# A scheduled state-space kernel: the scan pass's bfloat16 splits get a cost of their own in the planner

## The chip, the cores and the metric

The kernel runs on one core of a Trainium2 chip. The metric is the device time of one execution in microseconds (us). The core has five engines that run side by side, each with its own queue of instructions in order: TensorE (PE, matrix products and transposes), VectorE (DVE), ScalarE (ACT), GpSimd (POOL) and SyncE (SP), which issues the DMA transfers here.

## What is computed

A state-space image layer, followed by an attention and a quantized feed-forward layer, on `x` of 8 x 64 x 64 x 96. The scan pass, which the change touches, computes a selective scan over 4096 tokens in four directions (K = 4), for 192 channels, each with 16 states. Cut to what matters:

```
x_dbl = einsum('bkdl,kcd->bkcl', xs, x_proj_weight)       # 6 + 16 + 16 rows
dts, Bs, Cs = x_dbl[:, :, :6], x_dbl[:, :, 6:22], x_dbl[:, :, 22:]
delta = softplus(einsum('bkrl,kdr->bkdl', dts, dt_projs_weight) + bias)
h = h * exp(delta_t * A) + (delta_t * u_t) * B_t           # for each t, 16 states
y_t = sum over the states of h * C_t
y = y + D * u
```

Everything is float32. The rows `dts` and `Bs` enter matrix products as sums of three bfloat16 parts[...]: the first part is the value rounded to bfloat16, the second the rounded rest, the third the rest of that.

## The kernel before

There are three passes. Pass 1 normalizes, projects, convolves and makes `x_dbl`, which it stores as `xd_d`. Pass 2, the scan pass, is most of the time. Pass 3 is the gate, the attention and the feed-forward layer.

The order of instructions is not the order of the source. Each unit of work is a Python generator that, before each of its steps, yields an engine, an estimated cost in us, and sometimes a delay until the result can be used and a buffer that it needs. The function `weave` (from L142) plays the units against these costs: at each turn it takes, of all open units, the step that can begin first (`key = (max(begin, free[engine]), rank)`, ties by a rank that is a due time), and only then are its instructions written out. The engines later execute these lists in order; what the costs were then no longer plays a part, but the order that they made does.

The scan pass has 192 pieces: 4 pairs of batches, 3 channel groups c (two of 128 channels of one batch, and c = 2, which holds the last 64 channels of both), 4 directions k, and 4 stretches of T = 1024 tokens. A piece has 16 states n, each with these steps:

- ScalarE makes the decay `da` (exp of delta times A), in one of 3 buffers.
- The input term `dbu` is made in a PSUM buffer `wide` (3 of them) in one of three ways: ScalarE scales `duT` into `x` and TensorE transposes it; or GpSimd scales it into `xg` and TensorE transposes that; or TensorE spreads B over the partitions and VectorE multiplies by `du`.
- VectorE scans, two states into one `h` buffer (3 of them).
- GpSimd multiplies a pair of states by `c`, the rows of C that a DMA has spread over the partitions (6 buffers of 1 MB).
- TensorE transposes and sums the products into `acc`.

Once a piece, `prepare` loads the bfloat16 parts (`xdt`, `xb`) and `u`, and makes `delta`, `du` (GpSimd) and `duT`.

The generator `split` (L234) makes the three parts of `dts` and `Bs`. One split loads a tile `bq` of 128 x 512 (or 96 x 512) float32 from `xd_d`; ScalarE casts it into part 0 of `bs`; GpSimd subtracts that from `bq`; ScalarE casts the rest into part 1; GpSimd writes the last rest as part 2; SyncE stores `bs` in two transfers, into `b_d` or `dt_d`. Each batch needs 2 x 3 = 6 splits. Those of batches 0 to 4 (`b < LATE`, with LATE = 5) belong to pass 1 (L523) and have two buffers for each tile. Those of batches 5 to 7, 18 of them, are `late_split` units of the scan pass (L624 to 627) with one buffer each, one split open at a time, and a due time of five pieces for each split: the rank is `5 * N * (i + 1)`. They are wanted by the pieces of pair 2, which begin with piece 96 (`yield "split", b` in `prepare`).

The lines that the change and the prediction touch: the two `yield "pool", 4.4` in `split` (L245, L249), its signature (L234), and its two calls (L523, L626). The costs of the other steps on GpSimd in the scan pass are 4.55 for `times_c`, 2.5 for `scaled_by_pool` and 2.37 for `du`.

Of the kernel before, what the change touches and what calls it, by code (L numbers as in the profile page):

```python
# [230 lines left out]
    return a_neg, dsum, dt_b, dt_w, sel, sel2  # L231


def split(engines, pool_of, src, row, rows, pieces, at, dst):  # L234

    act, pool, sp = engines
    wide, used = GRP, rows * pieces
    yield "sp", 0.7, 4.0
    bq = pool_of.tile([P, wide], F32, name="bq")
    src = src[row : row + rows].rearrange("r (s t) -> (r s) t", s=pieces)  # L240
    sp.dma_start(bq[0:used], src[:, at : at + wide])
    yield "act", 0.6
    bs = pool_of.tile([P, NS, wide], BF16, name="bs")
    act.copy(bs[0:used, 0, :], bq[0:used])
    yield "pool", 4.4  # L245
    pool.tensor_sub(bq[0:used], bq[0:used], bs[0:used, 0, :])
    yield "act", 0.6
    act.copy(bs[0:used, 1, :], bq[0:used])
    yield "pool", 4.4  # L249
    pool.tensor_sub(bs[0:used, 2, :], bq[0:used], bs[0:used, 1, :])  # L250
    yield "sp", 0.9
    half = used // 2
    for k2 in range(2):
        to = dst[k2].rearrange("e n (s t) -> (n s) e t", s=pieces)[:, :, at : at + wide]
        sp.dma_start(to, bs[half * k2 : half * (k2 + 1)])


def splits(b, o, b_d, dt_d):

    return [(0, 2 * N, 4, at, b_d[b][o]) for at in (0, GRP)] + [(DT0, 2 * R, 8, 0, dt_d[b][o])]  # L260
# [3 lines left out]
def pass1(ctx, tc, g, consts, ident, mhalf, engines, u_d, z_d, xd_d, b_d, dt_d):  # L264
    nc = tc.nc
    pe, dve, act, pool = engines
    sp = InOrder(tc, nc.sync)
# [3 lines left out]
    two = ctx.enter_context(tc.tile_pool(name="p1two", bufs=2))  # L271
# [24 lines left out]
    def later_loads():  # L296
        load_by_type(act, conv_w, g["conv_w"])
        load_by_type(act, conv_b, g["conv_b"])
        w0 = 0
        for rows in (slice(R, R + N), slice(R + N, NXD), slice(0, R)):  # L300
            wide = rows.stop - rows.start
            for k2 in range(2):
                src = slice(k2 * NXD + rows.start, k2 * NXD + rows.stop)
                act.dma_start(w_xp[:, 0, :, w0 : w0 + wide], g["x_projT"][0:P, :, src])
                for j in range(2):
                    act.dma_start(w_xp[64 * j : 64 * j + 64, 1 + j, :, w0 : w0 + wide], g["x_projT"][P:DI, :, src])
                w0 += wide
# [28 lines left out]
    def statistics(b, q):  # L336
        if b > 1:
            yield "proj", b - 2
        yield "sp", 0.6, 4.0
        x = transposed(three, "xs", b, q)  # L340
        next(x)
        yield "pe", 0.7, 0.3, pts
        pt, slot = next(x), pts.taken
        end = yield "dve", 0.7
        if b not in sts:
            sts[b] = two.tile([C, NG, 6], F32, name="st")
        dve.bn_stats(sts[b][:, q, :], pt[0:C, :])
        pts.release(slot, end)
        one_more(("st", b), NG, end)

    def group_norm(b):

        yield "st", b
        yield "dve", 0.2
        mv = two.tile([C, 2], F32, name="mv")
        dve.bn_aggr(mv, sts[b].rearrange("p a b -> p (a b)"))
        yield "pe", 0.3, 0.3, mms
        pm, slot = ps_mm.tile([P, GRP], F32, name="pm", tag="mm"), mms.taken
        pe.matmul(pm[0:C, 0:1], gmat, mv[:, 0:1], start=True, stop=True)
        end = yield "dve", 0.5  # L360
        mms.release(slot, end)
        gm = wp.tile([C, 2], F32, name=f"gm{b}")
        dve.tensor_copy(gm[:, 0:1], pm[0:C, 0:1])
        dq = two.tile([C, 1], F32, name="dq")
        dve.tensor_sub(dq, mv[:, 0:1], gm[:, 0:1])
        dve.scalar_tensor_tensor(dq, dq, dq, mv[:, 1:2], ALU.mult, ALU.add)
        yield "pe", 0.3, 0.3, mms
        pv, slot = ps_mm.tile([P, GRP], F32, name="pv", tag="mm"), mms.taken
        pe.matmul(pv[0:C, 0:1], gmat, dq, start=True, stop=True)
        end = yield "dve", 0.2  # L370
        mms.release(slot, end)
        dve.tensor_copy(gm[:, 1:2], pv[0:C, 0:1])
        yield "pool", 1.0
        pool.tensor_scalar(gm[:, 1:2], gm[:, 1:2], 1e-5, None, ALU.add)
        pool.tensor_tensor(gm[:, 1:2], gm[:, 1:2], mhalf[0:C, 0:1], ALU.pow)
        end = yield "dve", 0.2
        dve.scalar_tensor_tensor(gm[:, 0:1], gm[:, 0:1], -1.0, gm[:, 1:2], ALU.mult, ALU.mult)
        gms[b] = gm
        done["stats", b] = end
# [98 lines left out]
    def x_projection(b, o, q):  # L478
        pair, j = b // 2, b % 2
        yield "u", pair, j  # L480
        yield "u", pair, 2
        px = None
        for ty, u in ((0, us[pair, j]), (1 + j, us[pair, 2])):
            end = yield ("pe", 0.62, 0.4) if px else ("pe", 0.62, 0.4, pxs)
            if px is None:
                px, slot = ps_px.tile([P, GRP], F32, name="px", tag="px"), pxs.taken
            if o == 0:
                src = u[:, q * GRP : (q + 1) * GRP]
            else:

                src = u.rearrange("p (h w) -> p h w", w=WW)[:, :, q * RPG : (q + 1) * RPG]
            pe.matmul(px, w_xp[:, ty, o, :], src, start=ty == 0, stop=ty > 0)
        one_more(("xproj", b), 2 * NG, end)
        by_dve = b == NB - 1 and q % 2 == 1
        end = yield ("dve" if by_dve else "act"), 0.6 if o == 0 else 0.8
        xd = four.tile([2 * NXD, GRP], F32, name="xd")
        src, dst = px[0 : 2 * NXD, :], xd
        if o == 1:
            src, dst = src.rearrange("p (h w) -> p w h", w=RPG), xd.rearrange("p (w h) -> p w h", w=RPG)
        (dve.tensor_copy if by_dve else act.copy)(dst, src)  # L500
        pxs.release(slot, end)
        end = yield "sp", 0.9, 3.0
        sp.dma_start(xd_d[b][o][:, q * GRP : (q + 1) * GRP], xd)
        one_more(("xd", b, o), NG, end)

    def after(key, unit):
        yield key
        yield from unit

    units = []  # L510
    for pair in range(NB // 2):
        batches = (2 * pair, 2 * pair + 1)
        for b in batches:
            units += [("stats", statistics(b, q)) for q in range(NG)]
            units.append(("norm", group_norm(b)))
            units += [("proj", projection(b, q)) for q in range(NG)]
        for c in ORDER:
            units.append(("conv", convolution(pair, c)))
        for b in batches:
            for o in range(2):  # L520
                units += [("xproj", x_projection(b, o, q)) for q in range(NG)]
                if b < LATE:
                    units += [("split", after(("xd", b, o), split((act, pool, sp), two, xd_d[b][o], *w))) for w in splits(b, o, b_d, dt_d)]  # L523
    later_loads()
    room = {"proj": 4, "norm": 1, "stats": 3, "xproj": 4, "split": 2, "conv": 3}
    weave([(kind, (list(room).index(kind), i), unit) for i, (kind, unit) in enumerate(units)], room, done)
# [3 lines left out]
def pass2(ctx, tc, g, ident, engines, fixed, u_d, xd_d, b_d, dt_d, y_d):  # L530
# [3 lines left out]
    pe, dve, act, pool = engines  # L534
    sp = InOrder(tc, nc.sync)
    one = ctx.enter_context(tc.tile_pool(name="p2one", bufs=1))
    two = ctx.enter_context(tc.tile_pool(name="p2two", bufs=2))
# [6 lines left out]
    pieces = [  # L544
        (pair, c, k, NPC - 1 - i if k >= 2 else i) for pair in range(NB // 2) for c in range(3) for k in range(K) for i in range(NPC)
    ]
# [6 lines left out]
    def one_more(key, of, end):  # L553
        counts[key] = counts.get(key, 0) + 1
        if counts[key] == of:
            done[key] = end
# [66 lines left out]

    def late_split(b, o, which):  # L624

        yield from split((act, pool, sp), one, xd_d[b][o], *which)  # L626
        one_more(("split", b), 6, 0.0)

    def load_c(at, m):
# [187 lines left out]
    units = []  # L817
    for at, (pair, c, k, pc) in enumerate(pieces):
# [21 lines left out]
        add("acc", 0, take_acc(at), N)  # L840
    last = [(b, o, w) for b in range(LATE, NB) for o in range(2) for w in splits(b, o, b_d, dt_d)]
    units += [("split", 5 * N * (i + 1), late_split(*which)) for i, which in enumerate(last)]
    weave(units, {"prep": 1, "c": 1, "da": 2, "x": 1, "xg": 1, "dbu": 2, "scan": 2, "carry": 1, "term": 1, "sum": 1, "acc": 1, "split": 1}, done)

# [285 lines left out]
```

## Time and profile before

| | us |
|---|---|
| median of 3 runs | 10572.03 |
| lowest and highest | 10562.71, 10575.15 |
| the profiled execution | 10581.88 |
| its span, first to last instruction | 10580.1 |
| scan pass in it, first scan to end of last scan | 762.6 to 9673.4 |

The page gives one profiled execution. A group line reads: line of the source (here always that of a helper, L91), engine, operation, output <- inputs, shapes, count | busy time in us, mean of one in ns | idle time of the engine just before, and what ended most of it. The view of stretches gives, for each, the length, and then for PE, the PE weight loads, DVE, ACT and POOL the busy time and the count, then the granted TensorE clock as a share of full speed, the DMA share and GB/s. A wait line reads: who waited <- for what: us in total, times, longest.

### The profile page before, as it was taken

The numbers are of one execution on the slowest core, as the hardware profiler recorded it, in microseconds if no ns is written. First come the engines' busy times: TensorE is split into PE (matmuls) and PEld (weight loads), VectorE is DVE, ScalarE is ACT, GpSimd is POOL, SyncE is SP. The second block draws the span as 40 slices with busy tenths as digits, with TensorE's granted clock in tenths as the row PEclk, the third lists the DMA queues.
The fourth block names the chain that finished last, engine by engine and source line by source line (L and its number), as shares of the span: only waits on it lengthen the run. The fifth ranks groups of instructions, "written<-read, shape, count | busy, mean of one in ns | idle before, by whom it ended". The sixth has DMA issues, their size and how long they took to land.

```text
span 10580.1 us, 151226 instructions
## 1 busy us (share of the span) xinstructions
PE 7655.9 (72%) x51232; PEld 6290.1 (59%) x51232; DVE 9604.6 (91%) x6918; ACT 9346.2 (88%) x21427; POOL 9230.7 (87%) x3271
## 2 busy tenths in 40 slices
PE   6857777766777777777677777777777777766887
PEld 3326666665566666666566666665566666655775
DVE  6869999988999999999999999999999999997776
ACT  5759999989999999999999999999999999996665
POOL 1539999988999999999999999999999999997886
PEclk8879898988889899988999999988999999897776
DMA  5766676678886666698966666899766667887442
GB/s 150 237 188 209 201 221 209 213 197 190 200 213 208 211 217 210 214 205 195 212 216 206 219 213 214 206 200 204 216 210 210 219 208 217 198 197 181 127 125 64
DMA packets 928007, 2103.20 MB, mean 199 GB/s; under 512 B 274391, under 2 KB 422648, under 8 KB 925700
## 3 DMA queue, kind: packets, MB, share of 16 engines
q1 hardware_dynamic: 919812, 2092.79, 70.8%
q8 instruction: 410, 6.72, 0.3%
q14 instruction: 361, 2.96, 0.1%
q10 hardware_dynamic: 7424, 0.74, 0.1%
HBM read 1917.59 MB, written 175.66 MB: 198 GB/s over the span
## 4 chain that ended last, share of the span: by engine, by line
ACT 29%; DVE 22%; issue 17%; PE 16%; POOL 11%; DMA 4%; SPq 1%; DVEq 0%; ACTq 0%; POOLq 0%
DVE h L91 16%; ACT x L91 13%; ACT da L91 11%; POOL c L91 7%; PE acc L91 6%; PE wide L91 6%; DVE wide L91 4%; PE mm L91 2%; ACT L91 1%; DMA xd_d<-xd 1%; DVE u L91 1%; ACT delta L91 1%; POOL xg L91 1%; PE pa L91 1%; ACT duT L91 1%
## 5 line engine op out<-in xcount | busy, mean ns | idle before, releaser
L91 POOL TENSOR_TENSOR c<-c,h 128x2048 f32<-128x2048 f32 x1536 | 6970.4, 4551 | 449.2 <-DVE h L91 380.8
L91 DVE TENSOR_TENSOR_SCAN h<-da,carry,wide 128x1024 f32<-128x1024 f32 x2304 | 5259.4, 2332 | 272.6 <-PE wide L91 187.6
L91 ACT ACTIVATE x<-duT,bT 128x128 f32<-128x128 f32 (+1 forms) x14336 | 4162.8, 367 | 45.9 <-PE wide L91 40.4
L91 ACT ACTIVATE da<-delta,a_neg 128x1024 f32<-128x1024 f32 x3072 | 3508.5, 1145 | 398.1 <-DVE h L91 385.7
L91 PE MATMUL acc<-ident,c 128*128 128x128 f32 x24576 | 3509.4, 300 | 466.5 <-POOL c L91 435.3
L91 PEld LDWEIGHTS acc<-ident,c 128*128 128x128 f32 x24576 | 3185.5, 156 | 780.9 <-POOL c L91 609.2
L91 PE MATMUL wide<-ident,x 128*128 128x128 f32 x11264 | 1631.5, 293 | 852.4 <-DVE h L91 826.9
L91 PEld LDWEIGHTS wide<-ident,x 128*128 128x128 f32 x11264 | 1358.7, 150 | 1150.2 <-DVE h L91 503.1
L91 DVE TENSOR_TENSOR_SCAN h<-da,wide 128x1024 f32<-128x1024 f32 x768 | 1710.0, 2272 | 128.9 <-PE wide L91 79.1
L91 DVE TENSOR_TENSOR wide<-du,wide 128x1024 f32<-128x1024 f32 x1216 | 1461.9, 1212 | 117.8 <-PE wide L91 115.9
L91 PE MATMUL wide<-xb,sel 96*128 96x512 bf16 x2432 | 763.3, 399 | 574.6 <-DVE h L91 491.4
L91 POOL TENSOR_TENSOR xg<-duT,bT 128x512 f32<-128x512 f32 (+1 forms) x640 | 892.2, 1409 | 57.6 <-PE wide L91 42.6
L91 PE MATMUL wide<-ident,xg 128*128 128x128 f32 x3584 | 519.3, 292 | 282.8 <-DVE h L91 273.1
L91 PEld LDWEIGHTS <-sel 96*128 96x128 bf16 x2432 | 225.1, 101 | 749.3 <-issue 366.9
L91 PEld LDWEIGHTS wide<-ident,xg 128*128 128x128 f32 x3584 | 431.1, 151 | 357.1 <-issue 203.6
L91 POOL TENSOR_TENSOR du<-delta,u 128x1024 f32<-128x1024 f32 x192 | 454.9, 2369 | 187.4 <-ACT delta L91 179.8
L91 ACT ACT_TABLE_LOAD x385 | 494.0, 1283 | 6.8
L91 DVE SCALAR_TENSOR_TENSOR u<-xpad,conv_w,u 128x4096 f32<-128x4096 f32 x96 | 459.1, 4782 | 1.9
L91 PE MATMUL px<-u,w_xp 128*128 128x512 f32 x512 | 255.7, 642 | 75.6 <-ACT u L91 45.4
L91 PE MATMUL mm<-w_out,gt 128*128 128x96 f32 (+1 forms) x1024 | 261.0, 375 | 35.0 <-POOL gt L91 16.3
L91 PE MATMUL wide<-ident,du 128*128 128x128 f32 x1536 | 212.4, 284 | 76.3 <-DVE h L91 53.5
L91 PEld LDWEIGHTS mm<-w_out,gt 128*128 128x128 f32 (+1 forms) x1024 | 199.9, 241 | 98.0 <-issue 31.7
(132 smaller groups left out, 5874.5 us busy)
## 6 DMA issues: line engine op xcount, KB each, us to landing
c<-xd_d SPq DMA_DIRECT2D x1024, 1024.0 KB
c<-xd_d SPq DMA_DIRECT2D x1024, 512.0 KB
u<-u_d SPq DMA_DIRECT2D x128, 512.0 KB
xdt<-dt_d SPq DMA_DIRECT2D x1152, 36.0 KB
xb<-b_d SPq DMA_DIRECT2D x384, 96.0 KB
u<-u_d SPq DMA_DIRECT2D x128, 256.0 KB
y_d<-y SPq DMA_DIRECT2D x24, 1024.0 KB
y<-y_d SPq DMA_DIRECT2D x64, 384.0 KB
```

The costliest lines, as they stand in the source:

```text
L91: ins = getattr(self.engine, op)(*args, **kwargs).ins
```

## The change

`split` takes the cost of its two GpSimd steps as an argument. Pass 1 gives the 4.4 that stood there; the scan pass gives 1.25. The instructions that `split` issues are the same.

```
-def split(engines, pool_of, src, row, rows, pieces, at, dst):
+def split(engines, pool_of, cost, src, row, rows, pieces, at, dst):
...
-    yield "pool", 4.4
+    yield "pool", cost
     pool.tensor_sub(bq[0:used], bq[0:used], bs[0:used, 0, :])
...
-    yield "pool", 4.4
+    yield "pool", cost
     pool.tensor_sub(bs[0:used, 2, :], bq[0:used], bs[0:used, 1, :])
...
-                    units += [("split", after(("xd", b, o), split((act, pool, sp), two, xd_d[b][o], *w))) for w in splits(b, o, b_d, dt_d)]
+                    units += [("split", after(("xd", b, o), split((act, pool, sp), two, 4.4, xd_d[b][o], *w))) for w in splits(b, o, b_d, dt_d)]
...
-        yield from split((act, pool, sp), one, xd_d[b][o], *which)
+        yield from split((act, pool, sp), one, 1.25, xd_d[b][o], *which)
```

## The prediction

> **What bounds the kernel now.** I read the page first, then the busy times of each engine in stretches, then the waits of VectorE in two of those stretches, then the groups that touch the split's tiles. From the page:
>
> ```profile
> PE 7655.9 (72%) x51232; PEld 6290.1 (59%) x51232; DVE 9604.6 (91%) x6918; ACT 9346.2 (88%) x21427; POOL 9230.7 (87%) x3271
> ...
> DVE 6869999988999999999999999999999999997776
> ...
> L91 POOL TENSOR_TENSOR c<-c,h 128x2048 f32<-128x2048 f32 x1536 | 6970.4, 4551 | 449.2 <-DVE h L91 380.8
> L91 DVE TENSOR_TENSOR_SCAN h<-da,carry,wide 128x1024 f32<-128x1024 f32 x2304 | 5259.4, 2332 | 272.6 <-PE wide L91 187.6
> ```
>
> Three engines are near 90% over the span, and the scan pass (slices 3 to 37) is flatter still. VectorE leads. The scan pass is 192 pieces of 16 scans, twelve stretches of 16 pieces: four pairs of batches, each with channel groups c = 0, 1, 2. I cut the trace at the first scan of each stretch (762.5 us for the first). The view of stretches, with the columns PE, PE loads, DVE, ACT, POOL (busy us and count), granted PE clock, DMA share and GB/s:
>
> ```profile
> 762.50:1505.20 742.70, 536.17 (x3818) 465.94 (x3819) 695.10 (x358) 690.91 (x1499) 686.47 (x187) 0.89 0.65 204
> 1505.20:2249.30 744.10, 540.66 (x3845) 474.42 (x3844) 698.74 (x361) 685.89 (x1496) 688.25 (x188) 0.88 0.68 211
> 2249.30:3051.60 802.30, 554.15 (x3754) 474.77 (x3753) 718.04 (x377) 744.52 (x1982) 723.59 (x249) 0.86 0.88 197
> 3051.60:3785.60 734.00, 526.74 (x3835) 454.82 (x3833) 694.91 (x361) 679.92 (x1473) 683.31 (x183) 0.91 0.68 212
> 3785.60:4505.90 720.30, 526.28 (x3841) 444.63 (x3840) 692.42 (x361) 677.93 (x1481) 676.70 (x178) 0.93 0.67 214
> 4505.90:5267.90 762.00, 543.36 (x3758) 459.89 (x3756) 715.34 (x377) 738.66 (x1971) 713.29 (x240) 0.89 0.90 203
> 5267.90:5989.30 721.40, 523.25 (x3834) 442.14 (x3835) 692.62 (x361) 675.79 (x1466) 676.33 (x177) 0.94 0.67 214
> ```
>
> The reader is to see that stretches 5, 6 and 7 repeat themselves: 720 to 722 us for c = 0 and 1, 762 us for c = 2, and the later pairs do the same. The first four are longer: by 742.7-720.3 = 22.4, 744.1-721.5 = 22.6 (721.5 is stretch 8), 802.3-762.0 = 40.3 and 734.0-720.4 = 13.6 (720.4 is stretch 10), together 98.9 us. VectorE's work in them is larger by only 2 to 6 us each; the rest is VectorE standing still. And these four are where the late splits are. The groups of the tile `bs` from 762.5 us on:
>
> ```profile
> L91 ACT CAST bs<-bq x35: 601/611/623, 767.8 to 3426.9; 128x512 bf16<-128x512 f32 x23, 96x512 bf16<-96x512 f32 x12
> ...
> L91 POOL TENSOR_TENSOR bs<-bq,bs x18: 1152/1167/1204, 768.5 to 3513.8; 128x512 bf16<-128x512 f32 x12, 96x512 bf16<-96x512 f32 x6
> ```
>
> The last subtraction is at 3513.8 us, inside the fourth stretch. A subtraction takes 1.17 us there (minimum 1152 ns, maximum 1204). VectorE's waits in the second stretch, and then in the fifth:
>
> ```profile
> DVE h L91 <- PE wide L91: 30.6, 16, 3.8
> ...
> DVE h L91 <- PE wide L91: 23.1, 15, 3.0
> ```
>
> VectorE waits for TensorE's transposes and never much for GpSimd itself; GpSimd reaches it through TensorE's queue, where a sum that waits for a product of GpSimd stands ahead of the next transpose.
>
> [...] beside the convolution of pass 1[...] the same subtraction has a median of 4.6 us (`bq`) and 3.5 us (`bs`); in the scan pass[...] it is 1.17. So 1.25 is about the real time and 4.4 is 3.2 us too long. [...]
>
> **The change part by part.** It removes no instruction and adds none: the 36 subtractions, 36 casts, 18 loads and 36 stores of the late splits stay as they are. It changes the planner's price of 36 subtractions from 4.4 to 1.25 us, so 36 x 3.15 = 113 us of GpSimd time that never existed leave the plan. What follows is an order of instructions, which can be compared without a run.
>
> Before, GpSimd's order puts these 36 in pieces 0 to 58, about one in every piece and a half. After, all 36 stand in pieces 0 to 17: four splits in the first two and a half pieces, and from piece 6 on almost exactly one split, two subtractions, to a piece. From piece 18 GpSimd's order is, piece for piece, the order that the kernel before has in pair 2 (pieces 96 to 143, the stretches of 721 to 762 us); VectorE's is so from piece 9. TensorE and ScalarE agree too, but for small swaps of neighbours of the kind that the kernel before also shows between its pairs 1 and 2, which cost nothing there (720.3 against 721.4 us). From piece 62 on both kernels have one order, the last pass included, but for a swap in piece 175.
>
> *What goes.* With the steady order, stretches 2 (from piece 18), 3 and 4 take steady times. All the excess of before, 98.9 us, is taken away, and the cost of 18 splits in pieces 0 to 17 is put in its place.
>
> *What a split costs in a piece.* GpSimd: 2 x 1.17 = 2.34 us. ScalarE: 2 casts of 0.61 = 1.22 us, and the wait of the first cast for its load, which stalled ScalarE 16.4 us in 7 of the 17 loads, so 1.0 us on average. A steady piece takes 720.3/16 = 45.0 us with GpSimd busy 42.3, ScalarE 42.4 and VectorE 43.3; so GpSimd goes to 44.6, ScalarE to 43.6, and none passes 45.0. The lower bound: in the steady stretch GpSimd waits 29.7 us for VectorE's `h`, 1.86 us a piece, and that idle time can take up all but 2.34-1.86 = 0.48 us. The upper bound: stretches 1, 2 and 4 of before have 26 subtractions and 58.6 us of excess, 4.5 us a split. I take GpSimd's own 2.34 us in full, ScalarE's part hidden under VectorE: VectorE and GpSimd hand `h` over in turn, so GpSimd's length passes on, while ScalarE runs two or three decays ahead. Cost 18 x 2.34 = 42.1 us. If ScalarE's cover went, 18 x (1.2+1.0) = 40 us more would show, which is the upper bound again.
>
> *SyncE's queue.* Each split moves one load of 256 or 192 KB and two stores of 192 or 144 KB, at most 0.64 MB; a piece moves 45 us at 214 GB/s, 9.6 MB. One split in each piece adds 7% to a DMA share of 0.67: hidden. The stores wait for the second subtraction, and the loads of `c` stand behind them; in the stretches of the splits SyncE waited 10.6 us for `bs` in all, 2016 us for buffers of `c`. That is covered.
>
> *Sum.* 98.9 - 42.1 = 56.8 us less. The profiled execution took 10581.9 us (span 10580.1), 9.9 above the median of 10572.0. Profiled: 10525.1. Median: 10515.2 us.
>
> **The rivals.**
> (a) The cost belongs to each subtraction and not to the wrong plan: 18 splits x 4.5 = 81 us remain, only the c = 2 stretch gains. 98.9-81 = 18 us less: 10554 us. For it: cut at every 16th scan, the pieces of stretch 1 without a subtraction take as long as steady ones. Against: in stretch 2 those without one are as long as those with one, and TensorE's order in the dense part after differs little from the steady order.
> (b) The splits vanish wholly in GpSimd's idle time: 18 x 0.48 = 8.6 us remain, 10482 us. For it: no engine is over 45.0 us in a piece. Against: GpSimd's waits for `h` need not fall where the subtraction stands.
> (c) Slower: ScalarE's queue is in order, and the cast stands ahead of the decays and scalings. At 2283.3 us of before, a cast waited 8.84 us for its load and VectorE stood still 6.76 us. In the dense part the next load goes out as soon as the stores of the last have been issued, into a queue that is filling the six `c` buffers. If each split did that, 18 x (6.76+2.34) = 164 us against 98.9: 10637 us. It decides from 98.9/18 = 5.5 us a split. Against: ten of 17 loads before kept nobody waiting, and the 8.84 was beside c = 2, with a DMA share of 0.88 to 0.90, where no split stands afterwards.
> (d) The order after reads steady and isn't, because TensorE's clock (0.88 in the split stretches, 0.93 later) belongs to the early time and not to the order: the stretches 2 to 4 stay long and the gain is at most the few us of DMA waits, so within 0.2%. Against: the clock rises just where the splits end.
>
> **How the numbers follow.** Forecast (costs from 1 to 3.5 us a split) 0.63; (a) 0.17; (b) 0.10; (c) 0.06; (d) 0.04. A measurement of this kernel tells about 0.2%, 21 us, from no change. Forecast and (b) are faster, 0.73, and with them somewhat over half of (a), 0.10: 0.83. The rest of (a) and (d): 0.11 the same. (c): 0.06 slower. The range of 8 in 10 goes from (b), 10480, to (a), 10553; (c), (d) and the far ends of (a) and (b) lie outside.
>
> **What would show it.** Stretches cut at every 256th scan: the third at 762, the fourth at 720 to 722, the second at 721.5 + 2 x 2.34 = 726, the first at 720.3 + 16 x 2.34 = 757.7; all later ones unchanged to 1 us. Subtractions of 1.15 to 1.20 us, the last before 1600 us. The clock of stretches 2 and 4 at 0.93. A first stretch of over 800 us, or casts that wait over 5 us each, would prove the forecast wrong; so would a third stretch near 800.

## The result, and the profile after

The changed kernel takes 10491.2 us (median of 4 runs, 10479.8 to 10496.2), against 10572.3 before: ratio 0.9923, 95% interval 0.9906 to 0.9941, 81 us less. The forecast was 10515.

The view of stretches after, cut at every 256th scan as before (us, then busy time and count of PE, PE loads, DVE, ACT, POOL, then clock, DMA share, GB/s):

```profile
764.50:1505.90 741.40, 542.38 (x3819) 465.53 (x3820) 693.78 (x359) 700.91 (x1526) 709.49 (x208) 0.89 0.69 215
1505.90:2227.50 721.60, 527.89 (x3848) 447.67 (x3847) 692.09 (x361) 679.08 (x1483) 680.83 (x182) 0.93 0.68 215
2227.50:2987.40 759.90, 532.52 (x3754) 447.96 (x3751) 714.22 (x377) 739.47 (x1974) 713.04 (x240) 0.91 0.91 203
2987.40:3707.20 719.80, 523.04 (x3828) 438.73 (x3829) 692.40 (x361) 676.42 (x1468) 676.15 (x177) 0.94 0.68 214
3707.20:4426.00 718.80, 527.80 (x3847) 446.35 (x3846) 692.30 (x361) 676.56 (x1478) 676.34 (x178) 0.93 0.67 214
```

The reader is to see that stretches 2, 3 and 4 have become steady ones, and that the first, which now holds 16 of the 18 splits, is no longer than it was (741.4 against 742.7). The first four stretches fell from 3023.0 to 2942.7 us, 80.3 us. The tile `bs` in the scan pass after:

```profile
L91 ACT CAST bs<-bq x35: 601/604/619, 769.2 to 1563.0; 128x512 bf16<-128x512 f32 x23, 96x512 bf16<-96x512 f32 x12
...
L91 POOL TENSOR_TENSOR bs<-bq,bs x18: 1150/1166/1217, 770.5 to 1577.2; 128x512 bf16<-128x512 f32 x12, 96x512 bf16<-96x512 f32 x6
...
  DMA bq<-xd_d: 3.9, 2
```

The subtractions are as long as they were and end at 1577 us instead of 3514; the casts waited 3.9 us for their loads in all, 16.4 before. On the page the work is the same and the idle time has gone:

```profile
PE 7609.8 (73%) x51232; PEld 6209.7 (59%) x51232; DVE 9588.2 (91%) x6918; ACT 9337.4 (89%) x21427; POOL 9214.1 (88%) x3271
```

VectorE's busy time is 16 us smaller, of 93 us that this profiled execution (10488.8 us) is shorter than the profiled one before. Of the 93 us, the first four stretches hold 80 and the eight later ones, which have the same order in both kernels, 10. So the difference holds some 12 us of chance: the execution of before lay 9.6 above its median, this one 2.4 below.

### The profile page after: what moved, and what is told of

Its sections match the earlier page's. It is cut to its first block, busy times and chain, and to the rows that moved or that the text cites. A ratio compares the mean times of both kernels' runs of the same rounds, so it can differ in the third digit from the quotient of the medians.

```text
span 10487.0 us, 151319 instructions
## 1 busy us (share of the span) xinstructions
PE 7609.8 (73%) x51232; PEld 6209.7 (59%) x51232; DVE 9588.2 (91%) x6918; ACT 9337.4 (89%) x21427; POOL 9214.1 (88%) x3271
## 4 chain that ended last, share of the span: by engine, by line
ACT 28%; DVE 21%; issue 18%; PE 16%; POOL 12%; DMA 4%; SPq 1%; ACTq 0%; DVEq 0%; POOLq 0%
DVE h L91 15%; ACT x L91 13%; ACT da L91 10%; POOL c L91 9%; PE acc L91 6%; PE wide L91 6%; DVE wide L91 3%; PE mm L91 2%; ACT L91 1%; POOL xg L91 1%; DMA xd_d<-xd 1%; DVE u L91 1%; DMA c<-xd_d 1%; PE px L91 1%; ACT delta L91 1%
## 5 line engine op out<-in xcount | busy, mean ns | idle before, releaser
L91 PEld LDWEIGHTS acc<-ident,c 128*128 128x128 f32 x24576 | 3145.3, 155 | 874.8 <-POOL c L91 737.0
L91 POOL TENSOR_TENSOR bs<-bq,bs 128x512 bf16<-128x512 f32 (+1 forms) x48 | 123.9, 2583 | 155.9 <-ACT bs L91 144.6
```

Source lines behind the costliest of these rows:

```text
L91: ins = getattr(self.engine, op)(*args, **kwargs).ins
```

## The experiments

The measure is the sum of the first four stretches of the scan pass, which hold all late splits. The run without a split in the scan pass (`late8`) gives the floor, 2920.1 us. All sums are from the profiled executions:

| kernel | price | pieces with subtractions | stretches 1 to 4, us | sum | over the floor |
|---|---|---|---|---|---|
| before | 4.4 | 0 to 58 | 742.7, 744.0, 802.3, 734.0 | 3023.0 | 102.9 |
| after | 1.25 | 0 to 17 | 741.4, 721.6, 759.9, 719.8 | 2942.7 | 22.6 |
| dense_4p4 | 4.4 | 0 to 18 | 760.6, 734.7, 760.0, 721.0 | 2976.3 | 56.2 |
| spread | 1.25 | 0 to 52 | 728.5, 718.3, 767.0, 726.3 | 2940.1 | 20.0 |
| price_2p8 | 2.8 | 0 to 30 | 750.7, 739.6, 763.7, 719.3 | 2973.3 | 53.2 |
| price_0p3 | 0.3 | 0 to 14 | 738.2, 720.1, 761.7, 719.9 | 2939.9 | 19.8 |
| late8 | none | none | 720.4, 719.1, 762.2, 718.5 | 2920.1 | 0 |
| ghost_4p4 | 4.4 | none, plan as before | 735.8, 737.2, 782.8, 733.4 | 2989.2 | 69.1 |
| ghost_1p25 | 1.25 | none, plan as after | 724.7, 721.3, 761.7, 719.9 | 2927.5 | 7.4 |
| triple | 1.25 | 0 to 31, 36 more | 730.2, 734.5, 759.6, 719.9 | 2944.2 | 24.1 |

`ghost_4p4` and `ghost_1p25` are the two kernels in which the splits are only booked, explained below. The six kernels from `price_2p8` to `triple` were executed once each. How much is chance can be seen from stretches 5 to 8, in which VectorE and GpSimd have the same order in all ten kernels: they sum to 2919.5 to 2925.2 us. A second profile of the changed kernel gave 2942.9 for stretches 1 to 4. So differences of a few us in the last column mean nothing.

**Price or place?** The change did two things at once: it made the price right, and it moved the splits from 58 pieces into 18. Two runs separate them. The first keeps the old price and makes the splits due earlier:

```
-        yield from split((act, pool, sp), one, 1.25, xd_d[b][o], *which)
+        yield from split((act, pool, sp), one, 4.4, xd_d[b][o], *which)
...
-    units += [("split", 5 * N * (i + 1), late_split(*which)) for i, which in enumerate(last)]
+    units += [("split", N * (i + 1), late_split(*which)) for i, which in enumerate(last)]
```

> The scan pass's price is 4.4 us again, but the due time of split i is one piece a split instead of five, so that its subtractions stand in pieces 0 to 18, as densely as in the changed kernel. Price theory (a wrong price makes a bad order wherever the split stands, 4.5 us a split as in the kernel before): first stretch 720 + 16 x 4.5 = 792 us, second about 730, third and fourth steady (760, 720), in all about 10550 us. Place theory (the price only decides where and for how long the splits stand; dense and early is cheap): first stretch 741, second 722, in all 10491 us, as the changed kernel.

Measured: 10528.4 us, ratio 0.9951 (0.9936 to 0.9965); first stretch 760.6. Neither theory has it: at nearly the same place the wrong price costs 56.2 - 22.6 = 34 us more than the right one, and yet 47 us less than in the kernel before. Part of the 34 is another stall, which the tile `bs` of this run shows among what its engines waited for:

```profile
  ACT bs L91: 48.3, 15
  DMA bq<-xd_d: 43.6, 15
```

Fifteen casts waited 2.9 us each for their loads, and fifteen subtractions for the casts. Probably, since with 4.4 us a subtraction the plan holds more time for a piece than the piece takes, the load is placed too late for the cast that follows it; no run isolates that.

The second run keeps the new price and holds the splits back:

```
     def late_split(i, b, o, which):
+        if i > 0:
+            yield "scans", 3 * i
         yield from split((act, pool, sp), one, 1.25, xd_d[b][o], *which)
```

> The price is 1.25 us, but split i may begin only when the scans of piece 3i are done, so that the subtractions stand in pieces 0 to 52, the c = 2 stretch included, about as in the kernel before. Price theory: 1.3 us a split wherever it stands, stretches 727, 728, 767, 724 us, in all about 10491 us. Place theory: the stretches of the kernel before, 742, 744, 802, 734 us, in all about 10572 us.

Measured: 10486.9 us, ratio 0.9913 (0.9897 to 0.993), sum 2940.1. With the right price the place makes no difference that can be told from chance: 20.0 us over the floor where the splits stand over 52 pieces, 22.6 where they stand in 18. So the place theory falls; and since place does matter at the wrong price (56 against 103 us), the price theory in its plain form, a fixed cost for each split, falls too.

> LATE = 8: all splits in the first pass, none in the scan pass. Both theories: stretches 1 to 4 at their steady 720, 721, 760, 720 us, which gives the floor against which a split's cost is measured (the changed kernel's first stretch is 741.4). If the first stretch stays above 730, part of the changed kernel's first-stretch excess belongs to the start of the pass and not to its splits. The first pass gets 36 subtractions more at 1.2 to 4.6 us each: the first scan later by 40 to 170 us if they are on its path, by less if GpSimd's idle time there takes them.

Its edit is one number:

```
-LATE = 5
+LATE = 8
```

Measured: 720.4, 719.1, 762.2 and 718.5 us, the floor; nothing of the first stretch belongs to the start of the pass. Its row:

```profile
810.40:1530.80 720.40, 522.13 (x3811) 445.04 (x3812) 692.34 (x361) 679.51 (x1486) 674.27 (x177) 0.93 0.66 210
```

The first scan begins at 810.4 us, 46 us later than in the changed kernel, and the whole takes 10513.8 us in its one execution: eighteen splits cost more beside the convolution, by those 46 us, than in the scan pass, 22.6 over the floor.

> The scan pass's price is 2.8 us, half way. The subtractions then stand in pieces 0 to 30. Price theory: the cost of a split lies half way between 1.3 and 4.5 or more, 18 x 2.9 = 52 us over the steady stretches 1 and 2 together, which is 28 us above the changed kernel, 10519 us. Place theory: no more than the changed kernel's 24 us if c < 2 and early is what counts, 10491 us.

Measured: 10529.2 us, sum 2973.3, 53.2 over the floor where the price theory had 52. As `dense_4p4` and `spread` refute that theory's fixed cost for each split, the agreement proves little. With `price_0p3` below and the due times of the kernel before, the cost by price is 20, 23, 53 and 103 us at 0.3, 1.25, 2.8 and 4.4 us; the place changes along with the price.

**Order or work?** What is it that costs, the order that the plan makes, or the splits' own instructions in it? In the next two kernels all splits are made in the first pass, and the late splits of the scan pass are booked in the plan and not written out:

```
-                if b < LATE:
+                if b < NB:
...
-        yield from split((act, pool, sp), one, 1.25, xd_d[b][o], *which)
+        yield "sp", 0.7, 4.0
+        yield "act", 0.6
+        yield "pool", 4.4
+        yield "act", 0.6
+        yield "pool", 4.4
+        yield "sp", 0.9
```

On VectorE, TensorE, ScalarE and GpSimd the order in all 192 pieces is that of the kernel before (or, with 1.25, of the changed one), less the splits.

> All splits are made in the first pass, and in the scan pass the late splits stay in the plan alone: the planner books their steps on SyncE, ScalarE and GpSimd at 4.4 us a subtraction, but no instruction is written out. Every engine's order in the scan pass is then the order of the kernel before, with the splits' own loads, casts, subtractions and stores left out (the results are the same). Order theory (the disturbed order costs by itself): the first four stretches stay near 740, 740, 790, 730 us, 60 to 90 us over the 2920 us of the run with no split in the scan pass. Work theory (the splits' own instructions, above all casts that wait for loads, make the cost in such an order): the four stretches fall to within 20 us of 2920.

> The same with 1.25 us: the order of the changed kernel with the splits' instructions left out of the scan pass. Order theory: 2920 to 2925 us in the first four stretches, and the changed kernel's 22 us over the floor are the work of its splits. If they stay at 2940, those 22 us too are the order's.

Measured: 69.1 us over the floor with the old plan, 7.4 with the new one, which is hardly more than chance. (As a whole they took 10600.9 and 10527.2 us; like `late8`, they make all splits in the first pass.) In the first four stretches of the kernel before, then, 69 of 103 us are lost with no split to execute: the order theory holds. Pieces 8 to 15 take 44.0, 46.9, 47.7, 49.0, 47.2, 45.5, 46.5 and 48.7 us in this run and the same to 0.1 us in the kernel before: there the splits themselves cost nothing at all. The rest, 102.9 - 69.1 = 34 us, comes with the splits' own instructions; 19.5 us of it stand in the third stretch, where in the kernel before one cast waited 8.84 us for its load. In the changed kernel the splits' work is 22.6 - 7.4 = 15 us, 0.84 us a split on average, but not evenly: the first piece takes 50.1 us there (48.4 in the second profile) against 43.2 with the splits only booked, so that it alone holds 5 to 7 of the 15 us.

The stretch rows of the two runs, the second stretch of each, first with the old plan and then with the new:

```profile
1550.20:2287.40 737.20, 537.30 (x3844) 470.17 (x3843) 698.71 (x362) 680.55 (x1486) 677.99 (x179) 0.89 0.68 210
```

```profile
1536.10:2257.30 721.20, 527.42 (x3835) 445.69 (x3834) 692.09 (x361) 679.12 (x1483) 676.24 (x178) 0.93 0.68 213
```

The same instructions, one order 16 us longer than the other. Of these 16, VectorE's idle time has 9.4 (38.5 against 29.1 us); its busy time has the other 6.6. In the traces of the two runs a scan alone takes 2.35 us, and three back to back 6.81; that this makes up the 6.6 us is my estimate. Only a part of the idle time is longer waits of the scans for TensorE. In the second stretch these waits are, first with the old plan and then with the new:

```profile
DVE h L91 <- PE wide L91: 26.2, 16, 2.8
```

```profile
DVE h L91 <- PE wide L91: 24.0, 15, 3.8
```

Over the four stretches the old plan is 61.7 us longer. VectorE's waits for TensorE's `wide` (by scans and by the products with `du`) have about 25 of this, 127.4 against 102.0 us, its waits for ScalarE about 13, its busy time 13, and pauses too short for the view the rest. So no single wait carries the cost.

What TensorE itself waited for shows how the order differs. It waited for GpSimd's products, in the second stretch, with the old plan and with the new:

```profile
PE acc L91 <- POOL c L91: 7.2, 8, 1.3
```

```profile
PE acc L91 <- POOL c L91: 27.2, 45, 1.5
```

With the old plan the products are ready when their sums come up in TensorE's queue; with the new one the sums stand further ahead and TensorE waits for them more. One place shows what can follow, the timeline of TensorE in piece 29 (start, length, what, count, in brackets the idle time before and who ended it). Old plan:

```profile
2165.99 0.60 PE L91 MATMUL wide<-xdt,dt_w 108*128 108x512 bf16 x2 [1.80 <-DVE h L91]
2166.43 3.17 PE L91 MATMUL acc<-ident,c 128*128 128x128 f32 x16
2169.39 1.49 PE L91 MATMUL wide<-ident,xg 128*128 128x128 f32 x8
```

and VectorE beside it:

```profile
2170.99 2.35 DVE L91 TENSOR_TENSOR_SCAN h<-da,carry,wide 128x1024 f32<-128x1024 f32 x1 [2.82 <-PE wide L91]
```

New plan, the same place:

```profile
2140.67 1.09 PE L91 MATMUL acc<-ident,c 128*128 128x128 f32 x8 [0.83 <-POOL c L91]
2141.64 0.61 PE L91 MATMUL wide<-xdt,dt_w 108*128 108x512 bf16 x2
2142.08 1.04 PE L91 MATMUL acc<-ident,c 128*128 128x128 f32 x8
2143.88 1.09 PE L91 MATMUL wide<-ident,xg 128*128 128x128 f32 x8 [0.76 <-DVE h L91]
```

```profile
2145.08 2.35 DVE L91 TENSOR_TENSOR_SCAN h<-da,carry,wide 128x1024 f32<-128x1024 f32 x1 [1.25 <-PE wide L91]
```

The scan waits for the transpose of `xg`. With the old plan all sixteen sums stand between the `dt_w` product and that transpose, and take 3.17 us; with the new one eight of them stand ahead of the product, in time that TensorE would have waited. VectorE then waits 2.82 us in place of 1.25. My reading, which the order fits but no run isolates: a plan that believes GpSimd late puts the sums late, and in the execution they are ready early and in the way.

A rival explains this place as well. TensorE's clock with the old plan, in three stretches of 3.4 us around it:

```profile
2163.50:2166.90 3.40, 1.59 (x18) 1.13 (x17) 3.40 (x3) 3.40 (x8) 2.34 (x2) 1.00 0.53 176
2166.90:2170.30 3.40, 3.40 (x19) 3.40 (x18) 1.27 (x1) 3.35 (x5) 3.40 (x1) 0.50 0.40 133
2170.30:2173.70 3.40, 1.77 (x15) 1.48 (x14) 2.71 (x2) 3.29 (x7) 2.86 (x3) 1.00 0.76 255
```

Most of the sums and of the transpose ran at half clock, 0.50. Sixteen sums took 1.91 us later in the same piece, and the next eight transposes 1.04. At these lengths the pair would have been 1.7 us shorter, which is more than the 1.57 us by which the wait grew. That the order costs 69 us is shown; which of its effects costs it, the sums in the way or the clock that goes with them, is not.

**Does GpSimd's own time pass on?**

```
     pool.tensor_sub(bs[0:used, 2, :], bq[0:used], bs[0:used, 1, :])
+    for _ in range(extra):
+        yield "pool", cost
+        pool.tensor_sub(bs[0:used, 2, :], bq[0:used], bs[0:used, 1, :])
```

with `extra` = 2 in the scan pass.

> In the scan pass the second subtraction is issued three times (the same result each time), each priced at 1.25 us: 36 more subtractions of 1.17 us, 42 us more GpSimd work in the split's pieces. If GpSimd's time passes on in full, the first four stretches are 42 us longer than the changed kernel's 2943; if it falls in GpSimd's idle time, under 10 us longer; at the 1.25 us a split measured so far against 2.34 us of work (about half), 20 us longer.

Measured: 2944.2 us, 1.5 more than the changed kernel, for 42 us more work. GpSimd's time doesn't pass on in full. The first two stretches of this run:

```profile
754.50:1484.60 730.10, 526.29 (x3821) 445.74 (x3822) 692.76 (x359) 693.89 (x1512) 715.47 (x215) 0.92 0.66 212
1484.60:2219.10 734.50, 528.98 (x3837) 448.71 (x3835) 693.14 (x361) 685.61 (x1496) 712.68 (x211) 0.92 0.68 216
```

In the second, GpSimd is busy 712.7 of 734.5 us, 36 us more than in a steady stretch, and VectorE's busy time is nearly unchanged. But that it is hidden wholly isn't shown. The edit changes the order too: the subtractions now reach to piece 31, the first stretch is 11 us shorter than in the changed kernel and the second 13 us longer. Counted from the floor, 72 subtractions, 84 us of work, cost 24 us in all.

**A price that is too low.**

> The scan pass's price is 0.3 us, 0.9 below the truth. The subtractions stand in pieces 0 to 14. If the size of the error in the price is what costs (36 x 0.9 = 32 us of GpSimd time missing from the plan, against 113 too much before), the first four stretches are 10 to 30 us longer than 2943. If only a price that is too high costs, because it leaves the engines less work in the plan than they can take, they stay at 2943 or below.

Measured: 10497.0 us, sum 2939.9, 2.8 us under the changed kernel. The edit is the number alone. An error of 0.9 us downward did no harm that shows here; 1.55 us upward (`price_2p8`) cost 31 us. So size alone doesn't decide; with one run on the low side I can't say how far down that holds. Nor does any run show why.

**Another price.**

```
-        end = yield "pool", 2.5, 0.2, slots["xg"]
+        end = yield "pool", 1.95, 0.2, slots["xg"]
```

> The changed kernel, and in it the other GpSimd step whose price is off: scaled_by_pool is planned at 2.5 us and takes 1.92 (1.88 from start to start), so 1.95 is written. It changes the order of every piece and not only of the first 18. If a price that is too high always costs as it did for the splits (about 0.6 us of stall for each us of false time, from 69 us in the run of the order alone against 113 us), the later stretches lose 2 x 0.55 x 0.6 = 0.7 us a piece, 10 us a stretch, 110 us in all, to about 10380 us. Rival: an error of 0.55 us, everywhere the same, leaves a regular order that already works (VectorE 96% busy in the steady stretches, its idle time 28 us of 720): the steady stretches stay within 3 us and the time within 20 us of 10491.

Measured: 10471.0 us, ratio 0.9904 (0.9887 to 0.992). The rival was nearer: stretches 5 to 12 sum to 5865.5 us against 5877.4, 1.5 us a stretch, and 110 us was far off. The gain is small but more than chance, since in the ten kernels of the table these stretches sum to 5875.3 at the least. The rate found for the splits doesn't carry over to a small error that is the same in each piece.

> Both together: splits at 1.25 us, one every three pieces, and scaled_by_pool at 1.95 us. If the two gains are separate, spread's 4 us less and the 20 us less of the other price: about 10467 us, first four stretches about 2930 us.

> The changed kernel once more, on the same chip as the run beside it, for the comparison: 10491 us, ratio 0.992.

Measured side by side: 10466.3 us, ratio 0.9898 (0.9883 to 0.9913), and 10494.1 us, ratio 0.9924 (0.9912 to 0.9937). The two prices and the held-back splits together are 28 us faster than the changed kernel beside them and 110 us faster than the kernel before (10576.2). From `xg_1p95` alone, ratio 0.9904, they can't be told apart.

## Why the prediction came out as it did

*The bound* was read rightly: VectorE leads, and what the first four stretches had over the later ones was idle time. Taking the later stretches as the floor, 98.9 us of excess, was 4 us short of what the run without splits gave, 102.9.

*The order.* The step that carried the forecast, that all pieces from 18 on take the steady order and with it the steady time, held: 721.6, 759.9 and 719.8 us, where 726, 762 and 720 to 722 were named. The later stretches moved by up to 3.3 us and not by at most 1, which is a scatter the text had not allowed for.

*The cost of a split* is the term that was mis-sized. The prediction charged GpSimd's 2.34 us in full, 42.1 us for 18, and named 757.7 us for the first stretch. It took 741.4. Over the floor the splits cost 22.6 us, 1.26 each; by the run with booked steps some 7 us of it are the order's and some 15 the work's. The reason given, that VectorE and GpSimd hand `h` over in turn so that GpSimd's length passes on, is what failed, in that it doesn't pass on in full: `triple` put 42 us more on GpSimd for 1.5 us. With 22.6 in place of 42.1, and 102.9 in place of 98.9, the sum is 80.3 us less, against 81 measured. Both misses went the same way, so the forecast of 57 us was too small and nothing cancelled.

*Rival (a)*, a cost that belongs to each subtraction, is refuted by the changed kernel, 22.6 us and not 81, and by the right price spread out, 20 us. *Rival (b)*, all hidden in GpSimd's idle time, was nearer than the forecast, 10482 against 10491 measured, but not right: 22.6 us remained where it had 8.6. *Rival (c)*, casts that wait for loads, did not occur in the changed kernel (3.9 us in all), but it is real: in `dense_4p4` it took 43.6 us of ScalarE's time. *Rival (d)*, a clock that belongs to the early time, fell: stretches 2 and 4 now run at 0.93 and 0.94.

What the prediction had not asked is why the old order was bad. It compared the orders, saw that one would be replaced by a known one, and needed no more. Its one remark on this, that a sum that waits for GpSimd's product holds up the next transpose, doesn't fit the runs with booked steps: with the old plan TensorE waited less for these products, 7.2 against 27.2 us in the second stretch. The sums stood in the queue ready, ahead of a transpose, in the place shown. Whether that or the clock makes most of the 69 us stays open.

## What to carry to other kernels

In a kernel whose order is written by a planner, a wrong price can cost through the order, not through its own length: here 36 steps booked at 4.4 us and taking 1.17 lost 69 us in queues where they weren't even executed. Not every wrong price does: one 0.9 us too low cost nothing that shows, and one 0.55 us too high in every piece cost 1.5 us a stretch. Look up what each step takes in the stage where it runs, since the same subtraction (`bq`, in the kernel before) had a median of 4.6 us in the first pass and 1.16 in the scan pass. To find what such a price is worth before correcting it, cut the trace at a unit of work that repeats and compare stretches with and without the step; to tell the order's cost from the step's own, book the step and leave it out.

## What the runs showed of the hardware

TensorE's granted clock differed with the order of the instructions. With the same matrix products the runs with booked steps had 0.89, 0.89, 0.89 and 0.90 in the first four stretches under the old plan and 0.91, 0.93, 0.90 and 0.94 under the new. Over the whole second stretch TensorE was busy 0.73 of the time under either plan (537.3 of 737.2 us and 527.4 of 721.2), so its mean load does not tell the two apart. Within a piece the clock changed too: it was 1.00, 0.50 and 1.00 in the three rows from piece 29. What in an order sets the clock is not shown.

In that place the sixteen sums took 3.17 us, most of it at the granted clock of 0.50, ahead of the transpose that the scan waited for; sixteen sums later in the same piece took 1.91 us. How much of the 69 us is the slower clock and how much the place of the sums, no run here separates.
